# Attention over row pairs: the sums over halves of the keys moved to GpSimd, and the output product moved into the second row's values bank, between the products for k and v

## The chip, the cores and the metric

The kernel runs on one core of a Trainium2 chip. The metric is the device time of one execution in microseconds, as the median of several runs. A profile is one further execution taken by the hardware profiler; its times are in microseconds from the start of its span.

## The reference, cut to what matters

The program computes four layers on an image of 256 x 256 pixels with 128 channels. The first is a row-wise attention with four heads of 32 channels; it is the only one that the change touches. After a layer norm it does, for every row of 256 pixels:

```python
q, k, v = (zn @ Wq), (zn @ Wk), (zn @ Wv)         # each split into H = 4 heads of C = 32
bias = zn @ Wb
g = sigmoid(zn @ Wg)
scores = einsum('bijhd,bikhd->bijkh', q, k) * (1.0 / C ** 0.5) + bias[:, None]
a = softmax(scores, axis=-2)                        # over the 256 keys of the row
o = einsum('bijkh,bikhd->bijhd', a, v)
out = (g * o).reshape(b, n, n, H * C) @ Wo
```

The kernel adds the result to its input, and collects sums and sums of squares for the norm of the next layer.

## The kernel before, in words

`attend_bounded` works through the 256 rows in 128 pairs; the variable `rp` counts pairs, and `a = 2*rp` and `b = 2*rp + 1` are a pair's two rows. Channels, or keys, lie on the 128 partitions, and a pair of rows is 512 columns wide. Everything in the loop is fp32. Every engine's instructions are pinned to the order in which the Python code issues them, so the order below is written by hand and no scheduler moves anything.

The loop is pipelined over pairs. While the loop body of `rp` runs, it computes the scores of the next pair, the projections of the pair after that, the weighted sums of the values for pair `rp`, and the output of pair `rp - 1`:

- `project(rp + 2, nm)` makes q, k, v and the gate g with TensorE (tiles ppq, ppk, ppv, ppg in PSUM). ScalarE moves each to SBUF (tq, tk, tv, tg); for the gate it takes exp(-x) on the way.
- `score(i)` makes the scores of one row, transposed, with the keys on the partitions: eight products into two PSUM tiles `sc`. `biased(i, p2)` adds the bias on VectorE (e<-sc,bT, two heads at a time, 1024 columns), and `exponent(i, p2)` takes the exponential on ScalarE, in place in e.
- A row has 256 keys, so e has two halves of 128. `fold(i)` adds the two halves into `ks` (1024 columns), so that the softmax's denominator takes one product per head and not two.
- `values(rp)` makes, for both rows, the weighted sum of the values (nd<-e,tv) and the denominators (nd<-ks,ones) in TensorE. The tile `nd` holds both rows and takes two PSUM banks.
- `gated(rp)` multiplies the denominator by 1 + exp(-g) into dn on VectorE; `inverse(rp)` takes its reciprocal as Ln and then Exp on ScalarE; `divide(rp)` multiplies the numerator with it into og on VectorE.
- `output(rp)` multiplies og with the output weights (px), adds the input on VectorE (x<-px,xr) with an accumulated sum, and every second pair sends x to memory by a DMA that the GpSimd queue issues. `squares(rp)` accumulates the squares on ScalarE (junk).

PSUM has eight banks. The two `sc` tiles in flight take four, `nd` takes two, and the last two are the two buffers of the tag `pj`, which ppq, ppk, ppv, ppg and px use in turn. ScalarE issues in the order Ln, Exp, tq, tk, tv, e, tg, e, junk, e, e in every pass of the loop. The inputs come by DMAs on the sync engine's queue, several pairs ahead.

All matrix products are recorded at line 60 (the helper `mm`), all activations at line 54, and all VectorE operations of this loop at line 576, where they are pinned. So the tiles' names tell the operations apart. The x DMA is at line 685.

Of the kernel before, what the change touches and what calls it, by code (L numbers as in the profile page):

```python
# [9 lines left out]
F32 = mybir.dt.float32  # L10
AF = mybir.ActivationFunctionType
ALU = mybir.AluOpType
# [5 lines left out]
P = 128  # L18
N = 256
NPIX = N * N  # L20
NCH = NPIX // 512
NH, HD = 4, 32
# [8 lines left out]
class Kernel:  # L31
# [27 lines left out]
    def mm(self, out, lhsT, rhs, start=True, stop=True):  # L59
        return self.nc.tensor.matmul(out, lhsT, rhs, start=start, stop=stop)  # L60
# [492 lines left out]
    def attend_bounded(self, xT, x1T, znT, bias, first, w, wo, stats1, shift1):  # L553


        nc, tc = self.nc, self.tc
        V = nc.vector
        with ExitStack() as c:
# [8 lines left out]
            ones = cp.tile([P, HD], F32, name="ones")  # L567
# [4 lines left out]
            pj = c.enter_context(self.pool(name="f3", bufs=3))  # L572
            hp = c.enter_context(self.pool(name="f4", bufs=2))
            ps = c.enter_context(self.pool(name="f5", bufs=2, space=PSUM))

            pin = lambda f: lambda *a, **k: tc.keep_in_program_order(f(*a, **k))  # L576
            mm, act_t, act_i = pin(self.mm), pin(act), pin(self.act)
            tt, stt, bn = pin(V.tensor_tensor), pin(V.scalar_tensor_tensor), pin(V.bn_stats)
            loaded, t, e, es, ks, nd, dn, og, x1s = {0: first}, {}, {}, {}, {}, {}, {}, {}, {}

            def chunk(rp):

                m = rp // 2
                if m not in loaded:
                    cols = slice(m * 1024, m * 1024 + 1024)
                    zn = io.tile([P, 1024], F32, name="zn2")
                    nc.sync.dma_start(zn, znT[:, cols])
                    xr = io.tile([P, 1024], F32, name="xr", bufs=3)
                    nc.sync.dma_start(xr, xT[:, cols])
                    loaded[m] = zn, xr  # L590
                s = slice((rp % 2) * 512, (rp % 2) * 512 + 512)
                return tuple(x[:, s] for x in loaded[m])

            def project(rp, nm):
                if rp >= N // 2:
                    return
                z = chunk(rp)[0]
                o = pj.tile([P, 4, P] if nm == "v" else [P, 512], F32, name="t" + nm)
                if nm == "v":
                    pv = ps.tile([P, 4, P], F32, name="ppv", tag="pj")  # L600
                    for ch in range(4):
                        mm(pv[:, ch, :], z[:, ch * P:(ch + 1) * P], w["v"])
                    act_i(o, pv, AF.Identity)
                else:
                    pp = ps.tile([P, 512], F32, name="pp" + nm, tag="pj")
                    mm(pp, w[nm], z)
                    if nm == "g":

                        act_t(o, pp, AF.Exp, scale=-1.0)
                    else:  # L610
                        act_i(o, pp, AF.Identity)
                t[rp, nm] = o

            def score(i):

                if i >= N:
                    return
                q, k, r = t[i // 2, "q"], t[i // 2, "k"], i % 2
                sc = [ps.tile([P, 2, 2, N], F32, name="sc", tag="sc") for _ in range(2)]
                for kc in range(2):  # L620
                    for h in range(NH):
                        hs = slice(h * HD, (h + 1) * HD)
                        mm(sc[h // 2][:, h % 2, kc, :], k[hs, r * N + kc * P:r * N + (kc + 1) * P],
                                q[hs, r * N:(r + 1) * N])
                for p2 in range(2):
                    e[i, p2] = sc[p2]

            def biased(i, p2):
                if i < N:
                    if not p2:  # L630
                        es[i] = hp.tile([P, NH, 2, N], F32, name="e", bufs=4)
                    hs = slice(2 * p2, 2 * p2 + 2)
                    tt(es[i][:, hs], e[i, p2], bT[:, hs], ALU.add)

            def exponent(i, p2):
                if i < N:
                    x = es[i][:, 2 * p2:2 * p2 + 2]
                    act_t(x, x, AF.Exp, scale=-1.0)

            def fold(i):  # L640

                x = ks[i] = hp.tile([P, NH, N], F32, name="ks")
                tt(x, es[i][:, :, 0], es[i][:, :, 1], ALU.add)

            def values(rp):

                v = t[rp, "v"]
                nd[rp] = ps.tile([P, 2, 2, N], F32, name="nd", **({"tag": "sc"} if rp == N // 2 - 1 else {"bufs": 1}))
                for r in range(2):
                    i = 2 * rp + r  # L650
                    for kc in range(2):
                        for h in range(NH):
                            hs = slice(h * HD, (h + 1) * HD)
                            mm(nd[rp][hs, r, 0], v[:, 2 * r + kc, hs], es[i][:, h, kc], start=kc == 0, stop=kc == 1)
                    for h in range(NH):
                        mm(nd[rp][h * HD:(h + 1) * HD, r, 1], ones, ks[i][:, h])

            def gated(rp):

                d = dn[rp] = hp.tile([P, 2, N], F32, name="dn")  # L660
                stt(d, t[rp, "g"].rearrange("p (r n) -> p r n", r=2), 1.0, nd[rp][:, :, 1], ALU.add, ALU.mult)

            def inverse(rp):
                if rp >= 0:
                    act_t(dn[rp], dn[rp], AF.Ln)
                    act_t(dn[rp], dn[rp], AF.Exp, scale=-1.0)

            def divide(rp):
                if rp >= 0:
                    og[rp] = pj.tile([P, 512], F32, name="og")  # L670
                    tt(og[rp].rearrange("p (r n) -> p r n", r=2), nd[rp][:, :, 0], dn[rp], ALU.mult)

            def output(rp):
                if rp < 0:
                    return
                xr = chunk(rp)[1]
                if rp % 2 == 0:
                    x1s[rp // 2] = io.tile([P, 1024], F32, name="x1")
                x1 = x1s[rp // 2]
                s = slice((rp % 2) * 512, (rp % 2) * 512 + 512)  # L680
                px = ps.tile([P, 512], F32, name="px", tag="pj")
                mm(px, wo["f"], og[rp])
                stt(x1[:, s], px, 1.0, xr, ALU.mult, ALU.add, accum_out=stats1[:, 0, rp:rp + 1])
                if rp % 2 == 1:
                    nc.gpsimd.dma_start(x1T[:, (rp - 1) * 512:(rp + 1) * 512], x1)

            def squares(rp):
                if rp >= 0:
                    junk = hp.tile([P, 512], F32, name="junk", bufs=1)
                    s = slice((rp % 2) * 512, (rp % 2) * 512 + 512)  # L690
                    act_t(junk, x1s[rp // 2][:, s], AF.Square, bias=shift1, accum_out=stats1[:, 1, rp:rp + 1])
# [20 lines left out]
                    exponent(i, p2)  # L712
            for rp in range(N // 2 - 1):
                a, b = 2 * rp, 2 * rp + 1
                score(a + 2)
                inverse(rp - 1)
                biased(a + 2, 0)
                biased(a + 2, 1)
                divide(rp - 1)
                for nm in "qkvg":  # L720
                    if nm == "g":
                        exponent(a + 2, 0)
                    project(rp + 2, nm)
                fold(a)
                fold(b)
                output(rp - 1)
                score(b + 2)
                exponent(a + 2, 1)
                squares(rp - 1)
                for p2 in range(2):  # L730
                    biased(b + 2, p2)
                    exponent(b + 2, p2)
                values(rp)
                gated(rp)

            rp = N // 2 - 1
            inverse(rp - 1)
            fold(N - 2)
            fold(N - 1)
            divide(rp - 1)  # L740
            values(rp)
            gated(rp)
            output(rp - 1)
            inverse(rp)
            squares(rp - 1)
            divide(rp)
            output(rp)
            squares(rp)

# [836 lines left out]
```

## Time and profile before

| what | value |
|---|---|
| median of 3 runs | 5087.27 us (5086.96 to 5087.37) |
| span of the profiled execution | 5083.0 us |
| PE busy | 4951.9 us (97%) |
| VectorE (DVE) busy | 4100.4 us (81%) |
| ScalarE (ACT) busy | 3496.8 us (69%) |
| GpSimd (POOL) busy | 406.9 us (8%) |
| e<-sc,bT on DVE | 512 of 1220 ns |
| ks<-e on DVE | 256 of 1217 ns |
| og<-nd,dn and dn<-tg,nd on DVE | 128 each, median 681 and 689 ns |
| e<-e on ACT | 512 of 1055 ns |

Busy times are sums over the whole span, over stages with different limits. Matmuls are pipelined and their ends are modelled, so a PE that is busy throughout need not be at its peak. A group's line gives busy time, mean duration, and the idle time of the engine just before, with the releaser that ended most of it. The chain of work that ended last tells which work set the time.

### The profile page before, as it was taken

What the parts mean: (1) busy time and instruction counts of PE and PEld (TensorE: products, weight loads), DVE (VectorE), ACT (ScalarE), POOL (GpSimd) and SP (SyncE); (2) the same over time, 40 slices, a digit from 0 to 9 for tenths busy, and PEclk for the clock granted to TensorE, in tenths of its full rate; (3) what the DMA queues carried; (4) which work ended last, traced back from release to release, by engine and by line L of the source; (5) the groups of instructions that cost most, each with busy time, mean ns of one, the idle gap of its engine ahead of it and who ended that gap; (6) DMA issues with size and microseconds to landing.
All of it is one profiled execution on the core that took longest, in us unless ns stands there. A gap on an engine that the chain in (4) does not pass through costs nothing.

```text
span 5083.0 us, 78992 instructions
## 1 busy us (share of the span) xinstructions
PE 4951.9 (97%) x31563; PEld 2715.8 (53%) x31563; DVE 4100.4 (81%) x4797; ACT 3496.8 (69%) x4948; POOL 406.9 (8%) x592
## 2 busy tenths in 40 slices
PE   8999999999999899999999999899999999999999
PEld 2444555555555333333333333329999953359999
DVE  6666999999999799999999999775333537779886
ACT  6445888888888899999999999453333357762110
POOL 0331000000000000000000000240111010000000
PEclk9999999999999999999999999999999999999999
DMA  8894222222222222222222221688667778865432
GB/s 290 292 338 173 88 80 84 84 80 88 84 80 84 68 68 68 72 64 76 64 73 67 72 68 60 218 324 309 237 229 243 252 286 321 324 233 180 142 122 67
DMA packets 204463, 781.69 MB, mean 154 GB/s; under 512 B 56278, under 2 KB 59628, under 8 KB 154788
## 3 DMA queue, kind: packets, MB, share of 16 engines
q1 hardware_dynamic: 146638, 505.57, 29.8%
q0 software_dynamic: 56160, 270.64, 14.8%
q8 instruction: 252, 4.13, 0.3%
q14 instruction: 117, 0.96, 0.1%
q10 hardware_dynamic: 1296, 0.40, 0.0%
HBM read 505.18 MB, written 271.32 MB: 153 GB/s over the span
## 4 chain that ended last, share of the span: by engine, by line
PE 57%; DVE 29%; issue 5%; ACT 1%; POOL 0%; DMA 0%; POOLq 0%; DVEq 0%; SPq 0%; ACTq 0%
PE z L60 9%; PE m L60 7%; PE nd L60 7%; PE sc L60 5%; PE zc L60 5%; PE po L60 4%; DVE tr L917 3%; DVE t L914 3%; DVE y L914 3%; DVE p L914 3%; DVE yf L914 3%; PE ppq L60 3%; PE ppv L60 2%; PE px L60 2%; PE pe L60 2%
## 5 line engine op out<-in xcount | busy, mean ns | idle before, releaser
L576 DVE TENSOR_TENSOR e<-sc,bT 128x1024 f32<-128x1024 f32 x512 | 603.1, 1220 | 49.8 <-PE sc L60 48.9
L54 ACT ACTIVATE e<-e 128x1024 f32<-128x1024 f32 x512 | 540.4, 1055 | 61.5 <-DVE e L576 52.4
L1077 DVE TENSOR_TENSOR LR<-z,sg 128x512 f32<-128x512 f32 x256 | 268.4, 1049 | 363.0 <-ACT sg L54 363.0
L60 PE MATMUL m<-U,v 128*128 128x128 f32 x4608 | 514.8, 275 | 0.0
L60 PEld LDWEIGHTS m<-U,v 128*128 128x128 f32 x4608 | 514.6, 192 | 0.0
L60 PE MATMUL z<-wf,zt 128*128 128x128 f32 x4096 | 459.6, 276 | 1.4 <-DVE zn L1077 1.4
L60 PEld LDWEIGHTS z<-wf,zt 128*128 128x128 f32 x4096 | 459.4, 192 | 2.3 <-DVE zn L1077 2.2
L54 ACT ACTIVATE sg<-z 128x512 f32<-128x512 f32 x256 | 152.9, 597 | 307.7 <-PE z L60 307.7
L54 ACT ACTIVATE sq<-zs 128x1024 f32<-128x1024 f32 x192 | 202.4, 1054 | 192.1 <-DVE zs L385 156.1
L576 DVE TENSOR_TENSOR ks<-e 128x1024 f32<-128x1024 f32 x256 | 301.0, 1217 | 0.0
L60 PE MATMUL sc<-tq,tk 32*128 32x256 f32 x4096 | 297.0, 401 | 3.0 <-DVE e L576 2.1
L60 PEld LDWEIGHTS sc<-tq,tk 32*128 32x128 f32 x4096 | 186.4, 184 | 159.6 <-issue 96.3
L60 PE MATMUL nd<-e,tv 128*32 128x256 f32 x4096 | 271.0, 382 | 0.0
L54 ACT ACTIVATE dn<-dn 128x512 f32<-128x512 f32 x384 | 241.9, 630 | 13.0 <-DVE dn L576 2.3
L60 PE MATMUL av<-y,ident 128*128 128x512 f32 x384 | 192.9, 611 | 44.0 <-DVE y L914 44.0
L60 PE MATMUL po<-LR 128*128 128x256 f32 x1024 | 222.2, 380 | 6.9 <-DVE LR L1077 6.9
L1462 ACT COPY m4s<-m 128x512 f32<-128x512 f32 x32 | 18.7, 583 | 287.2 <-PE m L60 287.2
L60 PEld LDWEIGHTS po<-LR 128*128 128x128 f32 x1024 | 194.1, 190 | 34.2 <-DVE LR L1077 7.7
L60 PE MATMUL bx<-p,ident 128*128 128x512 f32 x384 | 192.4, 610 | 0.0
L54 ACT ACTIVATE o<-po 128x256 f32<-128x256 f32 x256 | 84.3, 381 | 145.3 <-issue 110.5
L60 PEld LDWEIGHTS nd<-e,tv 128*32 128x32 f32 x4096 | 120.1, 109 | 108.2 <-issue 42.1
L889 ACT ACT_TABLE_LOAD x132 | 169.4, 1283 | 1.5
(366 smaller groups left out, 10321.1 us busy)
## 6 DMA issues: line engine op xcount, KB each, us to landing
zt<-znT SPq DMA_DIRECT2D x128, 1024.0 KB
znT<-zn POOLq DMA_DIRECT2D x64, 1024.0 KB, 5.2
xin<-x2T SPq DMA_DIRECT2D x64, 1024.0 KB
xin<-in_x_dram SPq DMA_DIRECT2D x50, 1024.0 KB
xr<-x3T SPq DMA_DIRECT2D x46, 768.0 KB
xT<-xo POOLq DMA_DIRECT2D x32, 1024.0 KB, 9.3
xr<-xT SPq DMA_DIRECT2D x64, 512.0 KB
zn<-znT SPq DMA_DIRECT2D x64, 512.0 KB
```

The lines of the kernel that those rows point to most:

```text
L54: return self.nc.scalar.activation(out, in_, func, bias=bias, scale=scale, **kw)
L60: return self.nc.tensor.matmul(out, lhsT, rhs, start=start, stop=stop)
L576: pin = lambda f: lambda *a, **k: tc.keep_in_program_order(f(*a, **k))
L889: pin(nc.scalar.preload_act_table_set(want))
L914: pin(V.tensor_tensor(out, a, b_, op))
L917: pin(V.scalar_tensor_tensor(out, a, k, b_, op0, op1))
L1077: pin = lambda f: lambda *a, **k: tc.keep_in_program_order(f(*a, **k))
L1462: nc.scalar.copy(m4, m[4])
```

## The change

There are four edits, all in `attend_bounded`.

1. `fold` uses GpSimd's tensor_tensor in the place of VectorE's, and both folds stand at the head of the loop body, before the scores of the next row.
2. `nd` becomes two tiles of one bank each, nd0 for the first row of the pair and nd1 for the second. `gated` and `divide` are each issued once per row, on 256 columns.
3. `divide(rp - 1)` stands between the two halves of `biased(a + 2, ...)`, and not after them.
4. `output(rp - 1)` is issued after the products for q and k of pair `rp + 2` and before those for v, and not after g. Its tile px no longer takes a `pj` buffer, but the bank of nd1 (for all but the last two pairs, which keep `pj`). So `pj` rotates through q, k, v and g alone.

The last pair's code after the loop is unchanged but for what the helpers do.

```diff
-            tt, stt, bn = pin(V.tensor_tensor), pin(V.scalar_tensor_tensor), pin(V.bn_stats)
+            tt, stt, add = pin(V.tensor_tensor), pin(V.scalar_tensor_tensor), pin(nc.gpsimd.tensor_tensor)
...
                 x = ks[i] = hp.tile([P, NH, N], F32, name="ks")
-                tt(x, es[i][:, :, 0], es[i][:, :, 1], ALU.add)
+                add(x, es[i][:, :, 0], es[i][:, :, 1], ALU.add)
...
-                nd[rp] = ps.tile([P, 2, 2, N], F32, name="nd", **({"tag": "sc"} if rp == N // 2 - 1 else {"bufs": 1}))
+                nd[rp] = [ps.tile([P, 2, N], F32, name=f"nd{r}", tag=f"nd{r}", bufs=1) for r in range(2)]
...
-                            mm(nd[rp][hs, r, 0], v[:, 2 * r + kc, hs], es[i][:, h, kc], start=kc == 0, stop=kc == 1)
+                            mm(nd[rp][r][hs, 0], v[:, 2 * r + kc, hs], es[i][:, h, kc], start=kc == 0, stop=kc == 1)
                     for h in range(NH):
-                        mm(nd[rp][h * HD:(h + 1) * HD, r, 1], ones, ks[i][:, h])
+                        mm(nd[rp][r][h * HD:(h + 1) * HD, 1], ones, ks[i][:, h])
...
-                stt(d, t[rp, "g"].rearrange("p (r n) -> p r n", r=2), 1.0, nd[rp][:, :, 1], ALU.add, ALU.mult)
+                for r in range(2):
+                    stt(d[:, r], t[rp, "g"][:, r * N:(r + 1) * N], 1.0, nd[rp][r][:, 1], ALU.add, ALU.mult)
...
-                    tt(og[rp].rearrange("p (r n) -> p r n", r=2), nd[rp][:, :, 0], dn[rp], ALU.mult)
+                    for r in range(2):
+                        tt(og[rp][:, r * N:(r + 1) * N], nd[rp][r][:, 0], dn[rp][:, r], ALU.mult)
...
-                px = ps.tile([P, 512], F32, name="px", tag="pj")
+                px = ps.tile([P, 512], F32, name="px", **({"tag": "nd1", "bufs": 1} if rp < N // 2 - 2 else {"tag": "pj"}))
...
             for rp in range(N // 2 - 1):
                 a, b = 2 * rp, 2 * rp + 1
+                fold(a)
+                fold(b)
                 score(a + 2)
                 inverse(rp - 1)
                 biased(a + 2, 0)
+                divide(rp - 1)
                 biased(a + 2, 1)
-                divide(rp - 1)
                 for nm in "qkvg":
+                    if nm == "v":
+                        output(rp - 1)
                     if nm == "g":
                         exponent(a + 2, 0)
                     project(rp + 2, nm)
-                fold(a)
-                fold(b)
-                output(rp - 1)
                 score(b + 2)
```

## The prediction

> **What bounds the kernel now.** I read the page's chain of work first, then the chain, timeline and waits inside the attention loop, which runs from about 457 to 1690 us of a 5083.0 us span; only this loop changes. The chain over one row pair (columns: start us, us, engine, tile, line, count):
>
> ```profile
> 1001.57 1.08 PE sc L60 x16
> 1002.64 1.06 PE ppq L60 x2
> 1003.70 0.86 PE ppk L60 x2
> 1004.56 0.99 PE ppv L60 x8
> 1005.54 0.86 PE ppg L60 x2
> 1006.40 0.95 PE px L60 x2
> 1007.36 1.08 PE sc L60 x16
> 1008.43 2.73 PE nd L60 x48
> ```
>
> All of it is TensorE. A pair takes 9.59 us (sc starts at 1001.50 and again at 1011.09 in the timeline). Equal work has unequal length here: ppk and ppg stand at 0.86, while ppv has 0.99 and px 0.95. By the spacing of its weight loads (eight in 0.97, the last 0.19 long) ppv is worth 0.89. So ppv holds 0.10 and px 0.09 of stall, 0.19 us a pair. The timeline says whose:
>
> ```profile
> 1002.68 2.36 DVE L576 TENSOR_TENSOR e<-sc,bT 128x1024 f32<-128x1024 f32 x2 [0.36 <-PE sc L60]
> 1004.38 0.97 PEld L60 LDWEIGHTS ppv<-rawv,zn 128*128 128x128 f32 x8 [0.66 <-ACT tq L54]
> 1004.95 0.68 DVE L576 TENSOR_TENSOR og<-nd,dn 128x512 f32<-128x512 f32 x1
> 1005.55 2.35 DVE L576 TENSOR_TENSOR ks<-e 128x1024 f32<-128x1024 f32 x2
> 1006.23 0.30 PEld L60 LDWEIGHTS px<-og,wo 128*128 128x128 f32 x2 [0.65 <-ACT tv L54]
> ```
>
> ppv waits for ScalarE to empty ppq's bank, px to empty ppv's: two PSUM buffers serve q, k, v, g and px in turn. The wait is nearly all hidden by the stream ahead; what shows is the weight load, issued too late to go in front (about 0.1 each). The DVE lines give its place: it starts when the scores are there, 1.18 after sc's start, and is idle 0.36 before. Its 9.2 us a pair do not set the 9.59:
>
> ```profile
> 700.00:1600.00 900.00, 900.00 (x9020) 475.79 (x9020) 828.63 (x939) 783.58 (x1127) 25.11 (x47) 1.00 0.27 84
> ```
>
> Over 900 us PE is busy 900.0, DVE 828.6 (92%), ACT 783.6 (87%), POOL 25.1; the clock is 1.00.
>
> **What the Trainium skill says.** "GPSIMD Engine Reference", section 3.1, gives a two-input fp32 add of 2048 elements as 4497 ns on GpSimd and 2293 on VectorE. The trace agrees on VectorE (1.22 us for 1024) and shows GpSimd only with one input. "SBUF — State Buffer", section "Who interferes with whom": a VectorE instruction with two SBUF inputs contends with a reading GpSimd instruction, one with at most one does not. The trace agrees where it can: in the first stage zn<-zs,pr (SBUF and PSUM) runs beside GpSimd's normalisation and stays at 1208 to 1222 ns. "Perfetto Trace Analysis", section "Tensor Engine Instruction (MATMUL, LD_WEIGHTS)": PE can pull a weight load ahead of matmuls in flight. ppk (0.86) against px (0.95) is that difference.
>
> **The change, part by part.** Times below are us from the start of sc(a+2) at 1001.50; 126 passes of the loop have the moved px.
>
> *Sums to GpSimd.* DVE loses 2 x 1.17 = 2.35 a pair. On GpSimd one is not in the trace: at least 1.19 (its one-input row), about 2.4 by the page (half of 4497 and some fixed cost; my value, an estimate), at most twice that. The first may start at -1.2, when the earlier sums have been read, and is needed near 7.8; the second is needed near 9.1. Up to about 4.7 each this costs nothing: values(rp) on PE is the cover. GpSimd's x1T issue (0.53, every second pair) stands between pairs of sums, waiting for x near 5.1; the next sum can't start before 8.6. DVE's freed time has no taker: the next scores come when PE gives them.
>
> *Two value tiles.* dn and og become two halves each. From 512 to 1024 columns DVE's pitch grows 0.60 to 1.14, so 256 columns are about 0.33 (0.41 until done): DVE gains 0.06 each. The first half of dn goes early; the second still waits for the last nd matmul and ends at 0.55 instead of 0.82. That saves nothing: the logarithm on ACT is behind e's last exponential anyhow. nd1 now waits for x, ready at about 5.1 and needed at 8.3: free.
>
> *px between k and v.* ppv's and px's old waits vanish (tq ends at 2.83, tk at 3.69, before they are needed): -0.19. The new wait is for og. Path over PE: first e starts 1.18, pitch 1.13, og's halves start at 2.31, the second ends 2.31 + 0.33 + 0.41 = 3.05. In the built program px waits for og in a semaphore instruction of its own, ahead of the matmul. For such a pair the trace shows 0.11 from end to weight load (y ends 2134.42, av's load 2134.53); a single wait takes 0.05. Load at 3.16, px through 0.96 later (0.10 exposed load, 0.86 stream), 4.12; ppv 0.89, ppg 0.86: 5.87. Before, px was through at 5.69 (its load at 1006.23, the same 0.96, less 1001.50). Thus **+0.18 a pair** (0.19 unrounded) even with the two old stalls gone. Behind px on PE stand ppv, ppg, both score products and nd: all shift.
>
> *The new loop through ScalarE.* This is what I add to it. ACT takes its work in order: Ln, Exp of dn, tq, tk, tv, e, tg, e, junk, e, e. tv is now behind px on PE, px behind og, og behind Exp. From tv's start, with the back-to-back pitches of the trace: e +0.49, tg +0.95, e +0.48, junk +0.95 (e's 1.05 less the usual overlap), its accumulator +0.63, e +0.19, e +0.95, Ln +0.95, Exp +0.66, its end +0.63: 6.88. Then og starts +0.03, ends +0.75 (0.33 + 0.41), px's load +0.11, px through +0.96, ppv's last result +1.06, tv +0.03: 9.82 to 9.84. So this ring alone takes **9.84** against 9.59, a little longer than PE's 9.78; with it px waits for og until 3.1 to 3.2. Delta 0.25 x 126 = **+31 us**. Bounds: if the extra semaphore costs 0.02, the accumulator 0.06 and the halves 0.02 less, the period is 9.70 (+14); with each 0.02 to 0.07 worse, 10.00 (+52).
>
> *Ends.* At the loop's end the last sum starts after the last exponential (1683.4) and ends near 1685.8 on GpSimd, 1685.2 before; the half dn gives 0.3 back: +0.4. Prologue: the first sums have 5 us of slack: nothing.
>
> Sum against the profile: 5083.0 + 31.4 = 5114.4 of span. The median of the runs, 5087.27, is 4.3 above the span, so about 5119.
>
> **Rivals.**
> 1. *The filler works: faster.* If og is there 0.1 before ppk has streamed (at 2.90), px costs no stall and the 0.19 is saved: -24 us, 5063. It decides at og's end by about 2.7; for it speaks only that the divide comes ahead of the second e. Against: scores at 1.15 plus one e of 1.13 leave no room for it before 3.05. With og ending near 2.87 the new stall equals the old ones: no change, 5087.
> 2. *GpSimd and VectorE hold each other up.* If a reading GpSimd blocks VectorE at its SBUF inputs, the second sum (about 1.2 to 3.6) lies on the first e and on og, right on px's path: 1 to 2.4 us a pair, 5215 to 5390. Against: the 1208 to 1222 ns above, and every DVE operation left in the loop has a PSUM input.
> 3. *GpSimd becomes the bound.* At 5 us a sum the period is 10 or more: 5140 and up. Against: the page's figure is half of it.
> 4. *The ring doesn't close*, ACT having more slack than I count: PE's path alone, +0.19 x 126 = +24, 5111; inside my own range.
>
> **How the numbers follow.** Slower by the wait for og, with or without the ring (5099 to 5140): 0.79. Held up by GpSimd (2 and 3): 0.05. The new stall about as large as the old: 0.07. Faster: 0.09. A measurement here tells about 0.2%, 10 us, from no change. So faster 0.09, same 0.07, slower 0.84. The likeliest case gives 5119; the range goes down to 5094, into the case of equal stalls, and up to 5146, where rival 3 begins.
>
> **What would show it.** Right: the pair at 9.75 to 9.95; px's weight load in the waits list behind DVE's og, 0.2 us or more late; ppv and ppg at 0.89 and 0.86 in the chain; ppv no longer behind tq; DVE's share in the loop down to about 70% with idle time ahead of og or e; ACT with its gap ahead of tv and none ahead of e, e. The sums at 2 to 3 us on POOL with no matmul waiting for them. Wrong: px's load without a wait (rival 1), DVE's e above 1.23 us (rival 2), nd waiting for ks (rival 3).

## The result and the profile after

The changed kernel takes **5118.57 us** (median of 4 runs, 5117.49 to 5119.43), the kernel before 5087.11 beside it: ratio 1.0062, with a 95% interval of 1.0048 to 1.0076. The profiled execution took 5117.76 us, with a span of 5115.5.

The added time is in the attention loop. From the first tq on ScalarE to the last it lasts 1252.7 us, against 1218.7 before: +34.0, while the span grew by 32.5. One pair, from one tq to the next, takes 9.863 us against 9.593 (medians): +0.270.

Three rows of the page of the kernel after: the busy times, and the groups of the first elementwise step and of the sums (busy us, mean ns of one | the engine's idle time just before, and what ended most of it).

```profile
PE 4956.4 (97%) x31563; PEld 2724.9 (53%) x31563; DVE 3842.0 (75%) x4797; ACT 3442.0 (67%) x4948; POOL 1010.9 (20%) x848
...
L576 DVE TENSOR_TENSOR e<-sc,bT 128x1024 f32<-128x1024 f32 x512 | 613.3, 1219 | 370.0 <-PE sc L60 367.0
L576 POOL TENSOR_TENSOR ks<-e 128x1024 f32<-128x1024 f32 x256 | 602.2, 2373 | 525.3 <-PE nd L60 507.4
```

The sums are on GpSimd, 2.37 us each, and VectorE's e is as long as before (1219 ns). VectorE is less busy, and waits more for scores. The same 900 us of the loop as before, in the stretch view of the kernel after (us, then the busy time of PE, weight loads, DVE, ACT and POOL, the granted clock, DMA share and GB/s):

```profile
700.00:1600.00 900.00, 879.14 (x8755) 469.63 (x8749) 621.61 (x912) 721.57 (x1095) 455.87 (x230) 1.00 0.26 81
```

DVE is down from 828.6 to 621.6 (69%), POOL up to 455.9. The line to look at is PE: 879.1 and not 900.0. TensorE now stands still inside the loop, 20.9 us of these 900. The chain of work of the kernel after, over most of a pair, shows where:

```profile
1203.46 1.15 PE sc L60 x16
1204.61 0.04 issue
1204.64 0.06 DVE e L576
1204.70 0.93 issue
1205.63 0.05 DVEq L576
1205.68 0.10 issue
1205.78 0.75 DVE og L576 x2
1206.54 0.14 issue
1206.67 1.10 PE px L60 x2
1207.77 0.89 PE ppv L60 x8
1208.66 0.86 PE ppg L60 x2
1209.52 1.08 PE sc L60 x16
```

Before, this chain went through TensorE alone: sc, ppq, ppk, ppv, ppg, px, sc. Now it leaves TensorE after sc, goes through VectorE (e, then og), and returns at px. From one sc to the next it was 1007.36 - 1001.57 = 5.79 us and is 1209.52 - 1203.46 = 6.06: the +0.27 of the pair. ppv is down from 0.99 to 0.89, as it should be once nothing stalls it; ppg stays at 0.86. The timeline of the kernel after has the same places as start and length (us, with the idle time before and its releaser in brackets; rows of other work between these are left out):

```profile
1203.39 1.15 PE L60 MATMUL sc<-tq,tk 32*128 32x256 f32 x16
...
1204.30 1.28 ACT L54 ACTIVATE dn<-dn 128x512 f32<-128x512 f32 x2
...
1204.64 1.23 DVE L576 TENSOR_TENSOR e<-sc,bT 128x1024 f32<-128x1024 f32 x1 [0.69 <-PE sc L60]
...
1205.78 0.74 DVE L576 TENSOR_TENSOR og<-nd,dn 128x256 f32<-128x256 f32 x2
...
1206.64 0.30 PEld L60 LDWEIGHTS px<-og,wo 128*128 128x128 f32 x2 [1.02 <-PE ppk L60]
1206.67 1.10 PE L60 MATMUL px<-og,wo 128*128 128x512 f32 x2 [0.22 <-DVE og L576]
```

Measured from sc's start at 1203.39: e starts at 1.25, og at 2.39, og ends at 3.13, and px's weight load starts at 3.25. The inverse on ScalarE (dn<-dn, Ln and Exp) ends at 1205.58, which is 0.20 before og starts: og waits for its turn behind e, not for the inverse. In the list of waits of the same 900 us (us in total, times, longest):

```profile
POOL ks L576 <- PE nd L60: 366.6, 91, 5.5
DVE e L576 <- PE sc L60: 261.9, 181, 2.2
ACT tv L54 <- PE ppv L60: 147.3, 91, 2.0
PEld px L60 <- PE ppk L60: 93.5, 91, 1.4
...
PE px L60 <- DVE og L576: 20.9, 91, 0.6
```

The waits of ppv for tq and of px for tv (0.66 and 0.65 us in the pair shown of before) are gone. 91 times, once a pair, px's matmul waits 0.23 for og. The weight load's long wait of about 1.03 is put down to ppk. But ppk was through at 1206.45 in the timeline of this pair, 0.19 before the load started, and og ended at 1206.52; what came last is og, as the chain says.

### The profile page after: what moved, and what is told of

Its sections match the earlier page's. It is cut to its first block, busy times and chain, and to the rows that moved or that the text cites. A ratio compares the mean times of both kernels' runs of the same rounds, so it can differ in the third digit from the quotient of the medians.

```text
span 5115.5 us, 79758 instructions
## 1 busy us (share of the span) xinstructions
PE 4956.4 (97%) x31563; PEld 2724.9 (53%) x31563; DVE 3842.0 (75%) x4797; ACT 3442.0 (67%) x4948; POOL 1010.9 (20%) x848
## 3 DMA queue, kind: packets, MB, share of 16 engines
q8 instruction: 252, 4.13, 0.3%
## 4 chain that ended last, share of the span: by engine, by line
PE 52%; DVE 30%; issue 8%; ACT 1%; POOL 0%; DVEq 0%; POOLq 0%; ACTq 0%
PE z L60 9%; PE m L60 7%; PE nd L60 7%; PE sc L60 6%; PE zc L60 5%; PE po L60 4%; DVE tr L920 3%; DVE t L917 3%; DVE y L917 3%; DVE p L917 3%; DVE yf L917 3%; PE px L60 3%; PE pe L60 2%; PE ppv L60 2%; PE ppg L60 2%
## 5 line engine op out<-in xcount | busy, mean ns | idle before, releaser
L576 DVE TENSOR_TENSOR e<-sc,bT 128x1024 f32<-128x1024 f32 x512 | 613.3, 1219 | 370.0 <-PE sc L60 367.0
L576 POOL TENSOR_TENSOR ks<-e 128x1024 f32<-128x1024 f32 x256 | 602.2, 2373 | 525.3 <-PE nd L60 507.4
L54 ACT ACTIVATE e<-e 128x1024 f32<-128x1024 f32 x512 | 525.4, 1051 | 8.2 <-DVE e L576 7.9
L1047 POOL DMA_DIRECT2D x2T<-x x64 | 34.2, 534 | 1493.3 <-ACT x L54 1493.3
L54 ACT ACTIVATE tv<-ppv 128x512 f32<-128x512 f32 x128 | 76.4, 597 | 202.9 <-PE ppv L60 202.9
L1212 POOL DMA_DIRECT2D prodD<-o x128 | 69.4, 542 | 617.1 <-ACT o L54 613.3
```

Source lines behind the costliest of these rows:

```text
L54: return self.nc.scalar.activation(out, in_, func, bias=bias, scale=scale, **kw)
L1047: nc.gpsimd.dma_start(x2T[:, b * 1024:(b + 1) * 1024], d["x2"])
L1212: nc.gpsimd.dma_start(prodD[g * CQ + d].rearrange("(p a j) -> p a j", p=P, a=2), o.rearrange("p a j b -> p a (j b)"))
```

## The experiments

All pair times are medians from tq to tq. Ratios are against the kernel before, run beside each one.

### The sums alone on GpSimd, in the kernel before

```diff
-                tt(x, es[i][:, :, 0], es[i][:, :, 1], ALU.add)
+                pin(nc.gpsimd.tensor_tensor)(x, es[i][:, :, 0], es[i][:, :, 1], ALU.add)
...
                 a, b = 2 * rp, 2 * rp + 1
+                fold(a)
+                fold(b)
                 score(a + 2)
...
-                fold(a)
-                fold(b)
                 output(rp - 1)
```

> The kernel before with one part of the change: the sums over halves on GpSimd, at the head of the loop; nd, divide and px as before. If px's wait for og is the whole cost, this costs nothing: 5087 us, within 3, the pair at 9.59 us, although each sum takes 2.37 us and VectorE loses 2.3 us a pair. If GpSimd's sums cost by holding VectorE up or by coming late, part of the 31 us shows here: 5095 to 5118. If freeing VectorE is worth anything by itself, it is under 5080.

Measured: 5086.84 us, ratio 1.000 (0.9991 to 1.0008); the pair stays at 9.593. The stretch from 700 to 1600 us of this kernel:

```profile
700.00:1600.00 900.00, 900.00 (x9015) 475.37 (x9014) 627.65 (x750) 770.49 (x1127) 467.33 (x235) 1.00 0.27 84
```

VectorE gave up 201 of 829 us, and PE is busy 900.0 of 900 as before. So a quarter of an engine's work was moved off, at no cost and for no gain: VectorE did not set the time. One thing did change. The first e of a pair starts 1.25 us after its scores (1205.63 against sc at 1204.38), and 1.18 in the kernel before (1204.14 against 1202.96). Here nobody waits for that.

### The changed kernel with the sums back on VectorE

```diff
-                add(x, es[i][:, :, 0], es[i][:, :, 1], ALU.add)
+                tt(x, es[i][:, :, 0], es[i][:, :, 1], ALU.add)
...
                 a, b = 2 * rp, 2 * rp + 1
-                fold(a)
-                fold(b)
                 score(a + 2)
...
                 biased(a + 2, 1)
+                fold(a)
+                fold(b)
```

> The changed kernel with the sums taken back to VectorE, after the second half of the bias addition; px stays between k and v in nd1's bank. If GpSimd's sums are the cost: back to 5087. If px's wait for og on PE's path sets the pair: nearly the changed kernel's time, but less the 0.07 us by which the first e starts later there behind an additional wait on GpSimd's semaphore (1.25 after sc's start, 1.18 before), so 9.79 us a pair and 5110 us. If the ring through ScalarE sets the pair, this 0.07 has no part in it: 5118.

Measured: 5115.23 us, ratio 1.0055 (1.0041 to 1.0068). The pair is 9.796, so 0.067 shorter than in the changed kernel. Two lines of its chain:

```profile
1200.36 1.09 PE sc L60 x16
...
1201.47 0.04 DVE e L576
```

e starts 1.11 after sc in the chain's count; in the changed kernel it is 1204.64 - 1203.46 = 1.18. The 0.07 is the whole difference of the pair. With the sums on VectorE it is 1.18 in the timeline (1201.47 against sc at 1200.29), with them on GpSimd 1.25, and every other run with e ahead of og falls on the same sides.

The waits in the trace show where the 0.07 is. In each of these kernels an instruction that only waits stands ahead of the first e. With the sums on VectorE, this one waits for an earlier result of VectorE, at 0.15 after sc's start (median), and the add itself waits for TensorE. With the sums on GpSimd, e's buffer was last read there, so the add has GpSimd to wait for as well; it takes that wait itself, and the wait for TensorE stands in the separate instruction. That instruction starts at 1.18, where the add would have started, and the add follows 0.066 later. GpSimd's own part was over by then: its last sum had ended 7.4 us before the add in the changed kernel (median), and 2.3 us before it even where each sum is made twice. So the 0.07 is the step from the separate wait to the add. What the two waits cost in the other order was not tried.

The total gained less than 126 x 0.067 = 8.4 us. In this profile the loop begins 2.3 us later and its tail is 4.5 us longer. The sums of the last pair stand on VectorE ahead of og, and TensorE waits 4.03 us for og at the end, where the changed kernel has 2.61. After this wait the granted clock is 0.54 (from 1712 to 1719 us, the last section comes back to it), and the products from here to px take 5.27 us instead of 2.72. So 1.4 us of the longer tail are the longer wait and about 2.5 the clock:

```profile
1712.62 1.93 PE L60 MATMUL nd<-e,tv 128*32 128x256 f32 x16 [4.03 <-DVE og L576]
```

### The squares cut short, in the changed kernel

```diff
-                    act_t(junk, x1s[rp // 2][:, s], AF.Square, bias=shift1, accum_out=stats1[:, 1, rp:rp + 1])
+                    act_t(junk[:, :32], x1s[rp // 2][:, s][:, :32], AF.Square, bias=shift1, accum_out=stats1[:, 1, rp:rp + 1])
```

> The changed kernel with the squares taken over 32 of a pair's 512 columns, so that ScalarE has some 0.4 us less to do between tv and Exp in every pair (the second moment of this stage is then another one). If the ring through ScalarE sets the pair, as predicted at 9.84, the pair falls to PE's own path: 5111 us or, with that path as the prediction has it, 9.78 a pair. If PE's path by e, og and px sets it, nothing moves: 9.86 a pair, 5118 us.

Measured: 5119.88 us, ratio 1.0064 (1.005 to 1.0078); the pair is 9.867. The kernel leaves out the squares of the other 480 columns, so its second moment is another one; only its time is of use. The inverse now ends 0.32 us before og starts, and not 0.20 (medians). ScalarE's work in the ring became shorter, and the pair did not: in the changed kernel the ring through ScalarE does not set the time.

### The output product after v, in the changed kernel

```diff
                 for nm in "qkvg":
-                    if nm == "v":
-                        output(rp - 1)
                     if nm == "g":
+                        output(rp - 1)
                         exponent(a + 2, 0)
```

> The changed kernel with the output product one place later, between the products for v and g; all else as changed. If the cost is that og is late for the place between k and v, it is there in time one product later: the wait is gone, px's old wait for tv is gone too since it has nd1's bank, and ppv waits for tq as in the kernel before: 9.50 us a pair, 5076 us, faster than both. If the halves of dn and og, the sums on GpSimd or the ring are the cost, it stays above 5100.

Measured: **5075.84 us**, ratio 0.9979 (0.9971 to 0.9987): faster than both kernels. The pair is 9.500. Its chain is back on TensorE throughout:

```profile
1204.62 1.08 PE sc L60 x16
1205.70 1.06 PE ppq L60 x2
1206.75 0.86 PE ppk L60 x2
1207.61 0.99 PE ppv L60 x8
1208.60 0.86 PE px L60 x2
1209.46 0.86 PE ppg L60 x2
1210.32 1.08 PE sc L60 x16
```

px is at 0.86 where it had 0.95 before the change; ppv has its 0.99 again, since it is once more close behind ppq and waits for tq. The pair is 9.593 - 0.093: px's part of the old stalls, and nothing else. One place further back in the issue order is enough to turn a loss of 31 us into a gain of 10.

### The output product after all four projections

```diff
                 for nm in "qkvg":
-                    if nm == "v":
-                        output(rp - 1)
...
                     project(rp + 2, nm)
+                output(rp - 1)
                 score(b + 2)
```

> The changed kernel with the output product at its old place, after g, but still in nd1's bank. This parts the place from the bank. If what makes the version with px after v fast is that px left the rotation of the two buffers (its old wait for tv, 0.09 us a pair), the place doesn't matter as long as og is there: 9.50 us a pair, 5076 us again. If it is the place, as something to fill a wait with, this is the kernel before again: 9.59 and 5087.

Measured: 5076.63 us, ratio 0.9979 (0.9969 to 0.9988), pair 9.500. This is the place that px had before the change; of px itself only the bank differs. So the new place is not needed for the gain, and it costs time if it is so early that og is not there. What is left is px's leaving the two buffers that the projections share. The sums have no part in it, as the run with the sums alone shows. The other edits, the halves of dn and og and the earlier division, were not taken out one by one, but the kernel before speaks against them: there og ends at 4.13 after sc's start, and px's weight load starts at 4.73, when tv is done. An earlier og could not have helped it.

### Each sum issued twice, in the changed kernel

```diff
-                add(x, es[i][:, :, 0], es[i][:, :, 1], ALU.add)
+                for _ in range(2):
+                    add(x, es[i][:, :, 0], es[i][:, :, 1], ALU.add)
```

> The changed kernel with every sum on GpSimd made twice into the same tile, so that its cost is doubled: 4.75 us each, 9.5 of a pair's 9.86. The prediction has them free up to about 4.7 each: nd waits for ks little or not at all, 9.86 to 10.0 a pair, 5118 to 5135 us. If the sums' cost or their traffic beside VectorE and PE were in the 31 us, this would add about as much again: 5150 and more.

Measured: 5126.5 us, ratio 1.0075 (1.0058 to 1.0092). The pair is 9.863, as in the changed kernel, although GpSimd now works back to back (4 x 2.37 = 9.5 us a pair). The additional 8 us are nearly all at the loop's end: from the last tq to the last px it takes 31.6 us against 24.4. There the chain runs through the sums on GpSimd, which have no later pair to hide behind; the two additional ones of the last pair are 2 x 2.37 = 4.7 us. In this profile the granted clock is also down, at 0.55 from 1727 to 1734 us: the last two px take 2.08 us each, against 1.12 and 1.13 in the changed kernel, which is 1.9 more. Inside the loop a sum of 4.7 us is still free.

### The division ahead of both halves of e

```diff
                 inverse(rp - 1)
-                biased(a + 2, 0)
                 divide(rp - 1)
+                biased(a + 2, 0)
                 biased(a + 2, 1)
```

> The changed kernel with the division ahead of both halves of the bias addition, so that og no longer waits for the first e, only for Exp on ScalarE. On PE's path alone og would be there 0.2 us sooner: 9.67 us a pair. But ScalarE's ring (Exp, og, px, ppv, tv, e, tg, e, junk, e, e, Ln, Exp) should lie just below the pair that was measured: Exp ends 0.08 us before og needs it there. So it takes over at 9.78 to 9.82: 5108 to 5113 us. Without a ring: 5094.

Measured: 5103.06 us, ratio 1.003 (1.0019 to 1.004); the pair is 9.704. The timeline of this kernel:

```profile
1203.42 1.28 ACT L54 ACTIVATE dn<-dn 128x512 f32<-128x512 f32 x2
...
1204.73 0.75 DVE L576 TENSOR_TENSOR og<-nd,dn 128x256 f32<-128x256 f32 x2 [1.66 <-ACT dn L54]
...
1207.65 0.60 ACT L54 ACTIVATE tv<-ppv 128x512 f32<-128x512 f32 x1 [1.45 <-PE ppv L60]
```

og no longer stands behind e. It now starts 0.03 after the inverse ends (1203.42 + 1.28 = 1204.70), as early as ScalarE permits. og ends at 2.97 after sc's start (1205.48 - 1202.51), against 3.13. And ScalarE waits 1.45 us for ppv ahead of tv, and then has no gap over 0.07 us up to the end of the next Exp, 6.75 us later (median). So the ring is closed: ppv stands behind px, px behind og, og behind Exp. The expectation with the ring was 9.78 to 9.82; the measured 9.704 lies between that and the 9.67 of a path without it.

### The same, with the squares cut short

```diff
-                    act_t(junk, x1s[rp // 2][:, s], AF.Square, bias=shift1, accum_out=stats1[:, 1, rp:rp + 1])
+                    act_t(junk[:, :32], x1s[rp // 2][:, s][:, :32], AF.Square, bias=shift1, accum_out=stats1[:, 1, rp:rp + 1])
```

> The division ahead of the bias addition, and the squares over 32 of a pair's 512 columns (another second moment), so both the first e and 0.37 us of ScalarE's work are out of px's way. If the ring sets the pair with the division first, this is faster than that one by 0.1 us or more a pair: 9.65 to 9.70, 5092 to 5100 us. If there is no ring, both are alike. Still slower than the kernel before, as og is late for its place all the same.

Measured: 5085.41 us, ratio 0.9998 (0.9989 to 1.0007); the pair is 9.588. Like the other run with few squares, this kernel leaves out most of the second moment.

That it would still be slower than before was wrong. The timeline of this kernel shows why:

```profile
1206.32 0.75 DVE L576 TENSOR_TENSOR og<-nd,dn 128x256 f32<-128x256 f32 x2 [1.55 <-ACT dn L54]
```

og ends 2.86 after sc's start (1204.21 in the same timeline). That is the point which the prediction named for a new stall as large as the old ones, 2.87 and 5087 us. The 9.67 that was expected of a path without the ring was too long. And the comparison answers the question of the ring: with the division first, shorter squares take 0.116 off the pair (9.704 to 9.588), and with the division behind e they took nothing off (9.863 to 9.867). The ring is there, at about 9.70. In the changed kernel it lies under TensorE's path of 9.86.

### The better place, with the sums back on VectorE

This is the kernel with px after v, and the sums on VectorE behind the second e:

```diff
                 for nm in "qkvg":
                     if nm == "g":
                         output(rp - 1)
...
                 biased(a + 2, 1)
+                fold(a)
+                fold(b)
```

> The changed kernel with the output product after v instead of between k and v (as in the run that took 5076), and with the sums over halves back on VectorE, behind the second e. Theory: what pays is px leaving the projections' two buffers; the sums on GpSimd only relieve VectorE, which has about 9.1 us of work a pair against a pair of 9.50 and so still fits. Then the pair stays at 9.50 and the total is about 5076 to 5082 (some us more at the loop's end, where the last pair's sums stand ahead of og on VectorE). Rival: with the shorter pair VectorE becomes the bound at its work plus its waits for the scores; then the pair is 9.55 to 9.65, nd waits for ks, and the total is 5085 to 5095: GpSimd's part would be needed for the gain.

Measured: 5077.69 us, ratio 0.9977 (0.9967 to 0.9988), pair 9.500. Its stretch from 700 to 1600 us:

```profile
700.00:1600.00 900.00, 900.00 (x9110) 487.91 (x9109) 840.84 (x1137) 781.85 (x1138) 25.62 (x48) 1.00 0.27 85
```

VectorE has 841 of 900 us, and PE still 900.0. So even the gain of the better version does not need GpSimd: moving the sums is worth nothing at either place.

## Why the prediction came out as it did

The total was forecast at 5119 and came out at 5118.57; slower had 0.84. The pair was forecast at 9.84 and came out at 9.863. The steps show that this agreement is partly luck.

- **Right: what bounds the kernel, and that VectorE's freed time has no taker.** The kernel with the sums alone on GpSimd stands at 1.000.
- **Right: the price of the sums.** They take 2.37 us, the estimate was 2.4 from "GPSIMD Engine Reference", section 3.1, and the trace agrees. The limit of about 4.7 us held too: sums issued twice left the pair at 9.863.
- **Right: no contention.** "SBUF — State Buffer", section "Who interferes with whom", says that a VectorE instruction with at most one SBUF input does not contend with GpSimd. The trace agrees: e has its 1219 ns beside sums that run 4.71 us in each pair.
- **Right: the old stalls go, and a new wait for og takes their place.** ppv and ppg are at 0.89 and 0.86; the halves of og took 0.74, as forecast, and from og's end to px's weight load it is 0.11.
- **Wrong: "first e starts 1.18".** This term of the path over PE was taken from the trace of before, as if moving the sums did not touch e. It starts at 1.25, because the buffer that e overwrites is now last read on GpSimd, and the wait for TensorE has moved into an instruction of its own. With 0.01 more in e's pitch and some thousandths at the weight load the path grew by 0.27 a pair, not by **+0.18**. The run with the sums back on VectorE shows it: 9.796, which is what the forecast's path of +0.19 gives with +0.01 for the pitch.
- **Wrong: "this ring alone takes 9.84".** The step that failed is the choice of what sets the pair. The ring's sum was too large: by 9.704 in the kernel where it does decide, it is about 0.14 smaller. In the changed kernel the way from tv's start to the Exp's end measures 6.74 (from 1208.70 to 1215.44), not 6.88; the largest part is the step from the squares' accumulator to e, 0.10 and not 0.19. Cutting the squares short, which shortens the ring, left the pair at 9.867.

So two errors of about 0.1 us with opposite signs met: the ring was over-sized by 0.14 and the path under-sized by 0.09, and the larger of the two numbers came out nearly the same, 9.84 and 9.86. The sign and the cause (px asks for og before VectorE can have it) do not rest on either. They rest on this: in all six kernels with px between k and v, the pair is og's end, counted from sc's start, plus 6.73 us (medians):

| kernel | og's end | pair |
|---|---|---|
| few squares | 3.138 | 9.867 |
| the changed kernel | 3.135 | 9.863 |
| each sum twice | 3.133 | 9.863 |
| sums back on VectorE | 3.067 | 9.796 |
| division first | 2.976 | 9.704 |
| division first, few squares | 2.859 | 9.588 |

What sets og's end differs: the first e on VectorE in the upper four, Exp on ScalarE in the lower two. With px after v og ends at 3.137 all the same, and the pair is 9.500: there px does not wait for it.

Rival 1, the filler that works, failed at the condition it named: og's end would have had to be at 2.7 and was at 3.13. Moved behind v, where og has been there for a while, the same product costs no stall; but of the 0.19 us of old stalls only the 0.09 of px is then saved, since ppv's wait for tq comes back. Of the 34 us in the loop, 126 x 0.27 accounts for all.

Two figures of the prediction do not come out of its own terms. "Its 9.2 us a pair" for VectorE is too large: 828.6 of 900 us, in a pair of 9.59, are 8.83. And three savings of 0.02, 0.06 and 0.02 from 9.84 give 9.74, not the lower bound of 9.70; the ring was then measured at 9.704, below what these terms allow.

The tail was forecast at +0.4. From the last tq to the last px it is 24.4 us against 23.8. The size is about right, its make-up is not: the last pair's nd used to take sc's banks, and in the changed kernel it waits 2.61 us for og, which has to read nd's banks first. TensorE's waits in this stretch are 3.04, 1.11 and 1.83 before and 2.14, 2.61 and 1.62 after, in sum 5.98 and 6.37. The first tq is 0.9 earlier after the change.

## What to carry to other kernels

An instruction that is put into a queue to fill another's wait must have its own input by then: work out its earliest time from the engine that makes it, not from the gap that it is to fill. If a tile's turn in a shared set of buffers is what causes the wait, give the tile another bank and leave its place alone. Moving the last reader of a buffer to another engine also gives the buffer's next writer one more engine to wait for, and which of its waits is split off is part of the price: here it was the one that comes last, and on a path with no slack even 0.07 us shows, 126 times.

## What the hardware showed unexpectedly

- **A late wait in an instruction of its own costs about 0.07 us.** The first e starts 1.25 us after sc in six kernels with the sums on GpSimd and 1.18 in three with them on VectorE (before, the sums back, px after v with the sums back; medians). In the six, the wait for TensorE stands alone, 0.066 us ahead of the add, although GpSimd's last sum had ended at least 2.3 us earlier (medians).
- **After a pause of TensorE at the loop's end, half clock can follow for some us.** In the kernel with the sums alone on GpSimd, TensorE waits 3.11 us for og there, and the two px products after it take 2.08 us in place of 1.13 in the kernel before. With px after v, a wait of 2.14 is followed by the same a little later, in the score products (2.07 us in place of 1.15). The granted clock (after the POOL column) of the two kernels, in the stretches after these waits:

```profile
1678.00:1684.00 6.00, 5.29 (x30) 2.31 (x34) 2.45 (x5) 1.89 (x4) 0.70 (x2) 0.50 0.17 72
```

```profile
1665.00:1668.50 3.50, 3.50 (x36) 1.93 (x40) 2.15 (x4) 1.84 (x4) 0.57 (x1) 0.52 0.37 150
```

  The clock is at 0.50 and 0.52 there, against 1.00 in the loop. "TensorE: Matmul & The Clock Gate", section "Part 1: The HAM clock gate (the "warmup" mystery)", describes this: the clock falls to half after a quiet window, and the windows run freely, whatever the program does. The traces fit in that the length of the wait alone does not decide: in the kernel before, a wait of 3.04 us at the same place, and in the changed kernel waits of 2.14 and 2.61, left the clock at 1.00. They differ from the page in the length: it gives an idle window of about 3.4 us, and here half clock followed a wait of 2.14 us. Busy time times the missing share of the clock gives an estimate of 2.6 and 1.7 us for the two stretches above, so it does not touch the comparison of the pairs, but it blurs comparisons of totals at this size. Whether it would vanish with other work put into the pause was not tried.
